# A merged stage of a graph layer: one more PSUM bank for the group's chain, paired product and rank tiles, a longer lead, and four-round turns without a barrier

## The chip, the cores and the metric

The kernel runs on one core of a Trainium2 chip. The metric is the device time of one execution in microseconds (us). The core has five engines that run their own instruction streams: PE (matrix multiply), DVE (vector), ACT (scalar and activation), POOL (GpSimd, which here issues indirect DMAs) and SP (which issues plain DMAs). They meet through semaphores alone. PE writes its results into PSUM, eight banks of 2 KB in each of 128 partitions; DVE and ACT read them from there.

## The reference

Two layers of a graph network over 32768 nodes with 256 features, and 524288 edges sorted by target:

```
# layer 0: attention inside blocks of 128 nodes (8 heads of 32), with residual
h  = relu(layernorm(x))
Q, K, V = (h @ W + b for W, b in ((Wq, bq), (Wk, bk), (Wv, bv)))
x  = x + softmax(Q @ K.T / sqrt(32) + edge_bias) @ V @ Wo + bo     # edge_bias lies in block 0 alone
# layer 1: one step of a gated graph layer, with residual
h  = relu(layernorm(x));  h = batchnorm(h)
a_in  = segment_sum((h @ W_in  + b_in )[src] * edge_weight[:, None],    dst)
a_out = segment_sum((h @ W_out + b_out)[dst] * edge_weight_n2[:, None], src)
xi, hh = concat(a_in, a_out) @ W_x2i + b_x2i,  h @ W_h2h
gate, new = sigmoid(xi[:, :256] + hh[:, :256]), tanh(xi[:, 256:] + hh[:, 256:])
x  = x + new + gate * (h - new)
```

The sums over edges are taken of the rows of h1 = relu(layernorm(x)) before the weights, which are applied afterwards.

## The kernel before

A first part of the program counts edges by block and builds tables of "items": an item is a window of 128 edges that have one target block of 128 nodes. Then comes the **merged stage**, which the change is about; after it, a stage that sums messages and rows by source and by target (`add_up`), and a last stage that computes the gates.

The merged stage does two things at once. One is layer 0: `project(g)` and `attend(g)` work on a group of four blocks (512 nodes). The other is to write, for every edge, the row of its target, scaled by the edge's weight, to the place that the edge has when sorted by source (`spread`, in three phases of edges, `PH`). Items are taken in rounds of 64 (`CI`). While a round runs, one group is attended and the next one projected; there are 64 groups, of which the first is done ahead.

For each item the steps are these (their lags in the table `steps`, line 1130, count items): `fetch` loads the target block's 128 rows `hb` from DRAM (SP). `spread_lanes` and `select` build a one-hot matrix `selT` from the edges' targets (PE, then DVE; once for four items), and `oh`, the one-hot of each edge's source block among 256 (DVE, one instruction for an item). `rank` (lines 1094 and 1096 to 1102) adds three bf16 products to a running count R in PSUM: `ones_b` with the oh of the item before, `triu` with that of two before, `tri` with its own. There are two tiles, R0 and R1, and items take them in turn. `place` (line 1114) is one DVE instruction that picks each edge's count out of R. `product` (line 1090) multiplies selT with hb into a tile `mp`, of which there are two. `scale` (line 1106, ACT) takes mp to SBUF with the edge's weight. `scatter` (line 1123, POOL) writes the 128 rows of 257 numbers and more to their places with an indirect DMA.

The **order** on PE, DVE, ACT and SP is that in which the Python loop over t emits instructions (`manual_schedule`, line 1139); POOL's is decided by the scheduler. At each t the loop emits the steps that are due by their lag and then what `project` and `attend` have registered for that t with the decorator `at(t)`. So their numbers are places in a common order: `at(B + 3)` stands behind the items' steps of t = B + 3. A wait is placed wherever an instruction needs a tile that another engine wrote, or writes a tile (or a PSUM bank) that another engine still reads.

PSUM is full: the group's chain has three tiles of one bank each, `sc`, `pt` and `mm`, which every part of project and attend shares; `bc` has one; mp two; R0 and R1 one each.

A **turn** is one passage of the hardware loop (`turns`, line 1135). Most turns hold four rounds (UG = 4), the rest of a phase takes turns of one round. At the end of a turn all engines meet at a barrier and their semaphores are reset. The loop of `add_up` does not do that: it is given `iteration_sync="staggered"`, its body is cut into four stages (`quarter`), and an engine may enter a stage when all have finished the stage before the last.

In the first phase there are five turns of four rounds, then turns of one round; in the second five; in the third four. Seven turns of one round have a group, and the last five have none.

Of the kernel before, what the change touches and what calls it, by code (L numbers as in the profile page):

```python
# [19 lines left out]
P = 128  # L20
# [479 lines left out]
def gnn_kernel(ctx, tc, x, src, dst, edge_attr, edge_type, w_in_e, w_out_e,  # L500
# [186 lines left out]
    with ExitStack() as c1:  # L687
# [56 lines left out]
        def project(g, qT, kbd):  # L744
# [7 lines left out]
            for b in range(GB):  # L752
# [7 lines left out]
                @at(17 + 2 * b)  # L760
                def _(b=b, row=row):
                    xn = row["xn"] = ab.tile([P, D], F32, name="xn")
                    nc.vector.tensor_scalar(xn, xg[:, b], mv[0][:, b, 0:1], rstd[0][:, b:b + 1],
                                            op0=ALU.subtract, op1=ALU.mult)

                @at(18 + 2 * b)
                def _(row=row):
                    row["tp"] = transposed("mm", row["xn"])

                @at(19 + 2 * b)  # L770
# [11 lines left out]
            for m in range(KC):  # L782
                ps = {}
                mc = slice(m * P, (m + 1) * P)
                bank = ("pt", "mm")[m]
                for k in range(KC):
                    @at(26 + 7 * m + k)
                    def _(m=m, k=k, ps=ps, mc=mc, bank=bank):
                        if k == 0:
                            ps["q"] = a_ps.tile([P, GN], F32, name=bank)  # L790
                        nc.tensor.matmul(ps["q"], wq[:, k, mc], hT[:, k], start=(k == 0), stop=(k == KC - 1))

                    @at(29 + 7 * m + k)
                    def _(m=m, k=k, ps=ps, mc=mc, bank=bank):
                        if k == 0:
                            ps["k"] = a_ps.tile([P, GN], F32, name=bank)
                        nc.tensor.matmul(ps["k"], wk[:, k, mc], hT[:, k], start=(k == 0), stop=(k == KC - 1))

                @at(28 + 7 * m)
# [3 lines left out]
                for j in range(HC):  # L803
                    @at(31 + 7 * m + j // 2)
# [10 lines left out]
            for b, t, bank in ((0, 41, "pt"), (2, 59, "sc")):  # L815
                ps = {}
                for i in range(2):
                    @at(t + i)
                    def _(b=b, i=i, ps=ps, bank=bank):
                        if i == 0:  # L820
                            ps["v"] = a_ps.tile([P, 2, D], F32, name=bank)
# [8 lines left out]
            @at(63)  # L830
# [5 lines left out]
        def attend(g, qT, kbd, bias=None):  # L836

            todo, at = steps_of()
            for b in range(GB):
# [3 lines left out]
                for m in range(KC):  # L843
                    hs = slice(m * HC, (m + 1) * HC)

                    @at(B + 4 * m)
# [7 lines left out]
                    @at(B + 1 + 4 * m)  # L854
# [5 lines left out]
                    for j in range(HC):  # L860
                        @at(B + (2, 6)[m] + j // 2)
# [3 lines left out]
                        @at(B + (3, 7)[m] + j // 2)  # L865
# [5 lines left out]
                    @at(B + (6, 9)[m])  # L871
# [7 lines left out]
                    @at(B + 10 + m)  # L879
# [7 lines left out]
                @at(B + 12)  # L887
# [6 lines left out]
                @at(B + 13)  # L894
# [3 lines left out]
                @at(B + 14)  # L898
# [4 lines left out]
                @at(B + 15)  # L903
# [5 lines left out]
                @at(B + 16)  # L909
# [9 lines left out]
                @at(B + 17)  # L919
# [3 lines left out]
                @at(B + 18)  # L923
# [5 lines left out]
                for n, u in enumerate(range(bs.start, bs.stop)):  # L929
                    h = {}  # L930

                    @at(B + 18 + 2 * n)
# [3 lines left out]
                    @at(B + 19 + 2 * n)  # L936
                    def _(u=u, h=h):
                        h["tp"] = transposed("mm", h1g[:, u])

                    @at(B + 20 + 2 * n)  # L940
# [3 lines left out]
            @at(B + 17)  # L944
# [3 lines left out]
            @at(B + 19)  # L948
# [3 lines left out]
            @at(B + 21)  # L952
# [26 lines left out]
        NM = 8  # L979
        fp = c1.enter_context(tc.tile_pool(name="p_f", bufs=1))  # L980
        wp = c1.enter_context(tc.tile_pool(name="p_w", bufs=2))
        sp = c1.enter_context(tc.tile_pool(name="p_s", bufs=2))
        op = c1.enter_context(tc.tile_pool(name="p_o", bufs=8))
        ip = c1.enter_context(tc.tile_pool(name="p_i", bufs=NM))
        hp = c1.enter_context(tc.tile_pool(name="p_h", bufs=10))
# [3 lines left out]
        zm = fp.tile([P, T3 // P, MW], F32, name="zmsg")  # L989
        nc.vector.memset(zm, 0.0)  # L990
        nc.vector.memset(zm[:, :, FW:FW + 1], -1.0e6)
        eno = fp.tile([CI, T1], F32, name="eno")
        nc.gpsimd.iota(eno, pattern=[[1, T1]], base=0, channel_multiplier=0, allow_small_or_imprecise_dtypes=True)
        R = [p1.tile([P, NB], F32, name=f"R{i}") for i in range(2)]
# [12 lines left out]
        def spread(k, lo, hi):  # L1007
# [8 lines left out]
            nc.scalar.dma_start(msg_d[k][hi - lo:hi - lo + T3].rearrange("(p e) w -> p e w", p=P), zm)  # L1016
            for r in R:
                nc.tensor.matmul(r, cn["row0"], soff[k], start=True, stop=False, skip_group_check=True)
# [69 lines left out]
            def product(i, q, c, turn):  # L1088
                mp = turn["mp", i] = pp.tile([P, D], F32, name="mp")
                nc.tensor.matmul(mp, turn["sel", i // 4][:, q % 4], turn.pop(("hb", i)), start=True, stop=True)  # L1090

            def add(what, of, to, turn):
                oh = turn["oh", of]
                nc.tensor.matmul(R[to % 2], cn[what], oh, start=False, stop=False, skip_group_check=True)  # L1094
# [15 lines left out]
            def place(i, q, c, turn):  # L1110
# [3 lines left out]
                nc.vector.scalar_tensor_tensor(jk, cn["iota1"], c["ed"][:, 0, q:q + 1], R[i % 2], op0=ALU.is_equal,  # L1114
# [331 lines left out]
```

## Time and profile before

| | us |
|---|---|
| median of 3 runs | 17105.49 (17104.96 to 17109.16) |
| profiled execution | 19598.35 |
| its span, first to last instruction | 19596.6 |
| first round of the merged stage begins | 1058.6 |
| last round with a group ends | 9421.7 |
| last scatter of the merged stage | 10044.9 |
| sums by source and target | 10064 to 17439 |
| gates, to the end | 17439 to 19597 |
| mean granted TensorE clock | 0.887 of full speed |

The profiled execution is one execution with the profiler on, and is longer than the timed ones. Times inside it are counted from its first instruction. In the page's part with the busy times, each engine has its busy time, its share of the span and its number of instructions; PEld is the loading of weights, which overlaps PE. The rows of digits cut the span in 40 slices, and PEclk is the clock that was granted, in tenths. A row of stretches gives, after the stretch and its length, the busy time and number of instructions of PE, PEld, DVE, ACT and POOL, then the granted clock, the share of the DMA engines and GB/s. A row of the waits names the waiting instruction and what released it, the total in us, how often, and the longest. A row in order of time gives start, duration, engine, line, operation, and in brackets the idle time before it with what ended that.

A round begins where the copies of line 1067 stand. Inside a turn of four rounds they are some 116, 122 and 129 us apart, and from the fourth round to the next turn's first some 152; turns of one round take 142 to 155 us with a group and 123 to 130 without.

### The profile page before, as it was taken

The numbers are of one execution on the slowest core, as the hardware profiler recorded it, in microseconds if no ns is written. First come the engines' busy times: TensorE is split into PE (matmuls) and PEld (weight loads), VectorE is DVE, ScalarE is ACT, GpSimd is POOL, SyncE is SP. The second block draws the span as 40 slices with busy tenths as digits, with TensorE's granted clock in tenths as the row PEclk, the third lists the DMA queues.
The fourth block names the chain that finished last, engine by engine and source line by source line (L and its number), as shares of the span: only waits on it lengthen the run. The fifth ranks groups of instructions, "written<-read, shape, count | busy, mean of one in ns | idle before, by whom it ended". The sixth has DMA issues, their size and how long they took to land. (4 is left out here: it accounts for less than half of the span.)

```text
span 19596.6 us, 292930 instructions
## 1 busy us (share of the span) xinstructions
PE 14917.0 (76%) x71786; PEld 10574.5 (54%) x71786; DVE 10035.6 (51%) x33823; ACT 6877.9 (35%) x17011; POOL 9326.3 (48%) x9309
## 2 busy tenths in 40 slices
PE   2078777777887777887668778777877777788889
PEld 2055555555555555555446666666666666653334
DVE  8656666566666656665444444444444444432222
ACT  0044444444444444444223333333333333320000
POOL 0045555445455445554555555555555555542222
PEclk6589989889888888988779999899999999999999
DMA  2044444444444434444446777677776777773332
GB/s 65 6 136 149 147 149 149 137 140 147 142 149 146 139 124 144 143 147 139 132 142 194 193 197 196 184 197 198 196 194 187 196 196 197 197 155 113 105 112 96
DMA packets 1829641, 2975.64 MB, mean 152 GB/s; under 512 B 299498, under 2 KB 1288135, under 8 KB 1827670
## 3 DMA queue, kind: packets, MB, share of 16 engines
q1 hardware_dynamic: 1203190, 1584.46, 27.5%
q0 software_dynamic: 430768, 1160.40, 20.5%
q10 hardware_dynamic: 194096, 212.95, 3.5%
q8 instruction: 590, 9.67, 0.2%
q14 instruction: 997, 8.17, 0.1%
HBM read 2124.16 MB, written 1248.64 MB: 172 GB/s over the span
## 5 line engine op out<-in xcount | busy, mean ns | idle before, releaser
L1123 POOL DMA_INDIRECT msg_d<-msg,pi x4352 | 4308.2, 990 | 3816.3 <-ACT msg L1106 1527.1
L1252 POOL DMA_INDIRECT rows<-h_d,ixc x3584 | 3407.5, 951 | 2331.8 <-issue 743.4
L1114 DVE SCALAR_TENSOR_TENSOR jk<-iota,edc,R 128x256 f32<-128x256 bf16 x4352 | 2072.8, 476 | 3059.3 <-remote 928.6
L1287 ACT ACTIVATE selo<-lane_row,sl 128x128 f32<-128x128 f32 x5040 | 1661.6, 391 | 4691.3 <-DVE sl L1284 1574.9
L1294 PE MATMUL ps_o<-m,selo 128*128 128x257 f32 x10080 | 2757.9, 413 | 645.7 <-ACT selo L1288 293.7
L1106 ACT ACTIVATE msg<-mp,edc 128x256 f32<-128x256 f32 x4352 | 2048.1, 477 | 3415.4 <-PE mp L1090 1522.5
L1266 PE MATMUL ps_i<-rows,sel 128*128 128x257 f32 x8960 | 2617.6, 412 | 761.6 <-DVE acc L1270 381.2
L1090 PE MATMUL mp<-hb,selT 128*128 128x256 f32 x8704 | 2926.6, 421 | 342.1 <-ACT msg L1106 145.7
L1294 PEld LDWEIGHTS ps_o<-m,selo 128*128 128x128 f32 x10080 | 1969.6, 205 | 1050.9 <-issue 312.5
L1266 PEld LDWEIGHTS ps_i<-rows,sel 128*128 128x128 f32 x8960 | 1627.5, 205 | 1054.7 <-DVE acc L1270 429.3
L1259 DVE TENSOR_SCALAR sel<-lane_row,ed 128x128 f32<-128x128 f32 x4480 | 1395.9, 360 | 973.2 <-PE idle L1267 374.7
L1090 PEld LDWEIGHTS mp<-hb,selT 128*128 128x128 f32 x8704 | 1460.2, 210 | 570.5 <-ACT msg L1106 230.9
L1094 PE MATMUL R<-oh,ones_b 128*128 128x256 bf16 x4352 | 1275.4, 293 | 635.6 <-issue 318.5
L1298 DVE SCALAR_TENSOR_TENSOR acc<-acc,blk,ps_o 128x257 f32<-128x257 f32 x1680 | 805.5, 479 | 1412.9 <-PE ps_o L1294 571.2
L1086 DVE TENSOR_SCALAR oh<-iota,edc 128x256 bf16<-128x256 bf16 x4352 | 1360.0, 313 | 2.0
L1094 PE MATMUL R<-oh,triu 128*128 128x256 bf16 x4352 | 1273.4, 293 | 10.5 <-DVE jk L1114 10.5
L1094 PE MATMUL R<-oh,tri 128*128 128x256 bf16 x4352 | 1272.2, 292 | 0.0
L1270 DVE SCALAR_TENSOR_TENSOR acc<-acc,blk,ps_i 128x257 f32<-128x257 f32 x2240 | 1070.0, 478 | 300.3 <-DMA sin_d<-acc 76.8
L1252 POOL DMA_INDIRECT rows<-h_d,ixh x896 | 852.2, 951 | 635.7 <-issue 247.2
L1284 DVE TENSOR_SCALAR sl<-m,blk 128x3 f32<-128x3 f32 x1680 | 416.6, 248 | 1372.4 <-DMA m<-msg_d 1139.5
L1094 PEld LDWEIGHTS <-triu 128*128 128x128 bf16 x4352 | 447.7, 103 | 1163.8 <-issue 1017.5
L1288 ACT ACTIVATE selo<-selo,one 128x384 f32<-128x384 f32 x1680 | 1031.1, 614 | 52.2
(372 smaller groups left out, 21051.9 us busy)
## 6 DMA issues: line engine op xcount, KB each, us to landing
m<-msg_d SPq DMA_DIRECT2D x1680, 396.0 KB
hb<-h_d SPq DMA_DIRECT2D x4352, 128.0 KB
sin_d<-acc SPq DMA_DIRECT2D x2240, 128.5 KB
sout_d<-acc SPq DMA_DIRECT2D x1680, 128.5 KB
msg_d<-msg,pi POOLq DMA_INDIRECT x4352
more<-sout_d ACTq DMA_DIRECT2D x128, 514.0 KB
rows<-h_d,ixc POOLq DMA_INDIRECT x3584
xg<-in_x SPq DMA_DIRECT2D x65, 512.0 KB
```

What stands on the lines that cost most here:

```text
L1086: nc.vector.tensor_scalar(oh, cn["iota1"], c["ed"][:, 0, q:q + 1], None, op0=ALU.is_equal)
L1090: nc.tensor.matmul(mp, turn["sel", i // 4][:, q % 4], turn.pop(("hb", i)), start=True, stop=True)
L1094: nc.tensor.matmul(R[to % 2], cn[what], oh, start=False, stop=False, skip_group_check=True)
L1106: nc.scalar.activation(msg[:, q % 4, 0:D], turn.pop(("mp", i)), AF.Copy, scale=c["ed"][:, 1, q:q + 1])
L1114: nc.vector.scalar_tensor_tensor(jk, cn["iota1"], c["ed"][:, 0, q:q + 1], R[i % 2], op0=ALU.is_equal, op1=ALU.mult, accum_out=c["pf"][:, q ...
L1123: s = nc.gpsimd.indirect_dma_start(out=msg_d[k][:], out_offset=bass.IndirectOffsetOnAxis(ap=c["pi"][:, j:j + 1], axis=0), in_=msgs[i // 4 ...
L1252: nc.gpsimd.indirect_dma_start(out=rows[(2 * i + r) % NR][:, 0:D], out_offset=None, in_=h1_d[:], in_offset=bass.IndirectOffsetOnAxis(ap=(i ...
L1259: nc.vector.tensor_scalar(sel[:, r], cn["lane_row"], c["ed"][:, 0, r, i:i + 1], c["ed"][:, 1, r, i:i + 1], op0=ALU.is_equal, op1=ALU.mult)
L1266: nc.tensor.matmul(ps, sel[:, r], rows[(2 * i + r) % NR], start=(r == 0), stop=(r == 1))
L1270: nc.vector.scalar_tensor_tensor(acc[0][i % NA], acc[0][(i - 1) % NA], c["blk"][:, 0, i:i + 1], c.pop(("t_ps", i)), op0=ALU.mult, op1=ALU.add)
L1287: nc.scalar.activation(sel[:, r], cn["lane_row"], AF.Abs, bias=sl[:, r:r + 1])
L1294: nc.tensor.matmul(ps, sel[:, r], m[:, r, 0:FW], start=(r == 0), stop=(r == T3 // P - 1))
```

## The change

It has five parts, all in the merged stage.

1. The group's chain gets a fourth PSUM tile, `mx`. The transposes of xn and h1g, and q, k and v of `project` use it; sc, pt and mm stay with attend. The numbers in `at()` are spread: between an instruction and the one on another engine that needs it there are now two steps where there was mostly one: sc at B + 5m (was 4m), av at B + 12 + m (was 10), o at B + 14 (was 12), its transposes at B + 16 (was 13), wo at B + 19 (was 15), x1g at B + 20 (was 16), std at B + 21, h1g at B + 23 + 3n (was 18 + 2n), its transposes at B + 25 + 3n, and k of project at 31 + 10m (was 29 + 7m).
2. mp becomes a tile for two items with two buffers (four items in two banks), and R0 and R1 become the halves of one tile in one bank. That is where the bank for mx comes from.
3. Items lead by 12 steps rather than 8: `LEAD`. There are 14 buffers for hb, not 10, and 7 for oh, not 8.
4. Turns of four rounds use the staggered form, with stage boundaries at each round's fourth step and without the hint for the branch. Turns of one round keep the barrier and the hint.
5. The row of zeros behind each phase's messages is kept once and broadcast by its DMA (three in all), and R is started by one matmul of 512 columns, not two of 256.

```diff
-                @at(17 + 2 * b)
+                @at(13 + 3 * b)
                 def _(b=b, row=row):
                     xn = row["xn"] = ab.tile([P, D], F32, name="xn")
...
-                @at(18 + 2 * b)
+                @at(15 + 3 * b)
                 def _(row=row):
-                    row["tp"] = transposed("mm", row["xn"])
+                    row["tp"] = transposed("mx", row["xn"])
...
-                    @at(26 + 7 * m + k)
-                    def _(m=m, k=k, ps=ps, mc=mc, bank=bank):
+                    @at(27 + 10 * m + k)
+                    def _(m=m, k=k, ps=ps, mc=mc):
                         if k == 0:
-                            ps["q"] = a_ps.tile([P, GN], F32, name=bank)
+                            ps["q"] = a_ps.tile([P, GN], F32, name="mx")
...
-            for b, t, bank in ((0, 41, "pt"), (2, 59, "sc")):
+            for b, t in ((0, 47), (2, 67)):
...
-            @at(63)
+            @at(67)
             def _():
                 nc.gpsimd.tensor_add(xb, xg, bo_b[:, None, :].to_broadcast([P, GB, D]))
...
-                        @at(B + (3, 7)[m] + j // 2)
+                        @at(B + 4 + 5 * m + j // 2)
                         def _(m=m, j=j, s=s):
                             if j == 0:
                                 s["pt", m] = a_ps.tile([P, HC, P], F32, name="pt")
...
-                @at(B + 16)
+                @at(B + 20)
                 def _(b=b, s=s):
                     nc.vector.tensor_add(x1g[:, b], s["y"], xb[:, b])
...
-                        h["tp"] = transposed("mm", h1g[:, u])
+                        h["tp"] = transposed("mx", h1g[:, u])
...
+        LEAD = 12
-        op = c1.enter_context(tc.tile_pool(name="p_o", bufs=8))
+        op = c1.enter_context(tc.tile_pool(name="p_o", bufs=7))
-        hp = c1.enter_context(tc.tile_pool(name="p_h", bufs=10))
+        hp = c1.enter_context(tc.tile_pool(name="p_h", bufs=14))
...
-        R = [p1.tile([P, NB], F32, name=f"R{i}") for i in range(2)]
+        R = p1.tile([P, 2, NB], F32, name="R")
...
             def product(i, q, c, turn):
-                mp = turn["mp", i] = pp.tile([P, D], F32, name="mp")
+                if i % 2 == 0:
+                    turn["mp"] = pp.tile([P, 2, D], F32, name="mp")
+                mp = turn["mp", i] = turn["mp"][:, i % 2]
...
-                nc.tensor.matmul(R[to % 2], cn[what], oh, start=False, stop=False, skip_group_check=True)
+                nc.tensor.matmul(R[:, to % 2], cn[what], oh, start=False, stop=False, skip_group_check=True)
...
-            steps = ((0, fetch), (4, spread_lanes), (6, select), (8, rank), (8, product), (8, place), (9, scale), (9, scatter))
+            steps = ((0, fetch), (LEAD - 4, spread_lanes), (LEAD - 2, select), (LEAD, rank), (LEAD, product), (LEAD, place),
+                     (LEAD + 1, scale), (LEAD + 1, scatter))
...
-                with tc.For_i(begin_at, end, nr, hint_engines=ENGINES) as it:
+                several = nr > 1
+                with tc.For_i(begin_at, end, nr, **({"iteration_sync": "staggered"} if several else {"hint_engines": ENGINES})) as it:
...
+                            if several:
+                                quarter(t, [0] + [i * CI + 3 for i in range(1, nr)], last + 1)
```

## The prediction

> **What bounds the kernel now.** I read the granted clock first (0.887), then the page's slices, the stretches, the chain, PE's waits, and last the order of time inside one round. The merged stage lies from 1058 us (its first round's copies) to 10045 us (its last scatter). Two lines of the page and one stretch, two steady rounds inside a turn, give its balance:
>
> ```profile
> PE 14917.0 (76%) x71786; PEld 10574.5 (54%) x71786; DVE 10035.6 (51%) x33823; ACT 6877.9 (35%) x17011; POOL 9326.3 (48%) x9309
> PEclk6589989889888888988779999899999999999999
> 1200.00:1460.00 260.00, 210.06 (x1156) 141.81 (x1155) 165.76 (x612) 122.76 (x307) 133.85 (x133) 0.91 0.48 152
> ```
>
> PE is busy 81% of the 260 us, DVE 64%, ACT 47%, POOL 51%: PE bounds the stage, with holes, and no second engine is near its limit. POOL sends scatters 1.29 us apart (0.99 busy, 0.30 issue) where an item takes about 2 us. The chain that ended last shows only the final stage (1% in all), so it says nothing here; the holes must be read from PE's waits over the 63 rounds with groups:
>
> ```profile
> PE R L1094 <- DVE jk L1114: 280.4, 201, 7.1
> PE R L1094 <- issue: 219.6, 116, 5.2
> PE sc L849 <- PEq L1135: 191.2, 15, 17.1
> PE pt L869 <- issue: 154.9, 90, 3.2
> PE mp L1090 <- ACT msg L1106: 136.4, 161, 2.3
> PE mm L741 <- DVE xn L763: 127.7, 39, 5.8
> PE mp L1090 <- issue: 93.5, 132, 2.4
> ...
> PE mp L1090 <- ACT kbd L810: 61.8, 56, 1.8
> ```
>
> ("issue" is a wait whose release the trace did not keep; an instruction's "issue" rows are counted with its named ones.) Three families: the rank waiting for the place (280.4 + 219.6 = 500 us), the barrier (191), and the links of the group's chain and of the product (L741 311 us with its smaller rows, L869 272, L1090 292: 875 us). Inside a round, at full clock:
>
> ```profile
> 1612.07 0.27 PE L1094 MATMUL R<-oh,ones_b 128*128 128x256 bf16 x1
> ...
> 1612.29 0.27 PE L1094 MATMUL R<-oh,tri 128*128 128x256 bf16 x1
> ...
> 1612.39 0.60 PE L1090 MATMUL mp<-hb,selT 128*128 128x256 f32 x2
> ...
> 1612.60 0.48 DVE L1114 SCALAR_TENSOR_TENSOR jk<-iota,edc,R 128x256 f32<-128x256 bf16 x1 [1.31 <-PE R L1094]
> ...
> 1612.83 0.27 PE L1094 MATMUL R<-oh,ones_b 128*128 128x256 bf16 x1
> ...
> 1613.00 0.08 DVE L1114 DVE_READ_ACCUMULATOR jk<-iota,edc,R 128x1 f32 x1
> ```
>
> An item costs PE 0.76 us (12.07 to 12.83). DVE's place starts 0.04 us after the rank's last matmul and is done at 13.08, 1.01 us after the rank began. Here the next rank began 0.25 us before that: it writes the other R tile.
>
> **Pages against the trace.** "PSUM — Partial Sum Buffer", section "PSUM bank collisions raise a hardware error", says that two engines on one bank and the same partitions at once are an error, whatever columns they touch, so that such instructions are ordered. In the rows above PE writes one R tile while DVE reads the other, which is allowed as they lie in different banks. The changed kernel puts both halves in one bank, and its built program does what the page says: a rank's first matmul waits for the place of the item just before, where it now waits for the one two back. The forecast goes by the page. The second is "TensorE: Matmul & The Clock Gate", Part 1: PE falls to half clock after an idle window of about 3.4 us. The trace agrees: after the 10.84 us hole at a turn's end the first R matmul (at 1588.00) takes 0.40 us, and one at 1589.61 takes 0.27. I take no gain from it in the sum.
>
> **The change part by part** (profiled execution, 19598.35 us, span 19596.6).
>
> 1. *Longer links in project and attend, and the bank mx.* xn to its transposes was one step and is two; exp to transposes likewise; h1g, o and wo likewise; xn, q, k, v and h1 get a bank that attend's mm, pt and sc do not share. The work itself is the same. The product's two buffers become two pairs: by the built program the even product waits for the scale three items back, the odd one for no scale. These are the 875 us. With the lock of part 2 DVE is at most one step behind PE, so a DVE link two steps long is met without a wait. ACT may be three behind and keeps its 1.28 us table loads and its waits for DVE's kbd (430.7 us on ACT), and the first steps of a turn have no items to cover a link. I keep a third: -583 us. From both sides: -780 (only a tenth stays) and -437 (half stays).
>
> 2. *R in one bank.* Lower side of the cost: a rank can follow the one before by 1.09 us at the soonest (1.01 and 0.04 to each side) instead of 0.76. In the turns' 4011 neighbours 955 are closer than 1.1 us, by 260 us together. Upper side: item by item the larger of PE's work, DVE's work and 1.1 us, which sums to 120.5 us a round, against PE's own 102.9 (both from the trace's durations between ranks and between places): 17.6 us a round. In between stands what each place really allows, as DVE may begin its step while PE is still in the step before: the sum of 1.09 plus DVE's work less PE's work of two steps, where positive. It is 11.7 us a round; with three steps, today's case, 0.6. With the changed order of steps (work lists of both programs, 13.1 against 14.3) it becomes 10.7. Today's waits are 500/63 = 7.9, so 7.3 a round come from lateness that such sums miss (DVE held by its own links); half of it goes with part 1. After: 10.7 + 3.7 = 14.4 a round, 907 us over 63 rounds: +407 us.
>
> 3. *No barrier between turns of four rounds.* 14 such turns in three runs of 5, 5 and 4, so 11 edges. Today an edge leaves PE idle for 10.84 us:
>
> ```profile
> 1570.12 0.37 PE L1094 MATMUL R<-oh,triu 128*128 128x256 bf16 x1 [0.21 <-DVE jk L1114]
> 1581.32 2.07 PE L849 MATMUL sc<-kbd,qT 128*128 128x512 f32 x2 [10.84 <-PEq L1135]
> ```
>
> The next stage's loop already passes its edge by stages, and there PE has a hole of 5.11 us:
>
> ```profile
> 10621.30 0.39 PE L1267 MATMUL idle<-lane_row,sel 128*128 128x128 f32 x2
> 10626.80 2.94 PE L1294 MATMUL ps_o<-m,selo 128*128 128x257 f32 x6 [5.11 <-ACT selo L1288]
> ```
>
> So 11 x 5.7 = -63 us. The hint for the branch goes with the barrier; its price is inside that 5.11. The stage waits stand 14 steps behind each boundary, when the awaited work is long done: nothing. They are also in POOL's and SP's queues. POOL may lag 32 items by its eight message buffers, less than the 50 steps allowed.
>
> 4. *Lead of 12, seven oh, 14 hb.* SP issues the same DMAs (hb 128 KB each), four steps earlier against the product; 14 buffers against 12 leave SP two steps ahead, as 10 against 8 did. SP's xg load now stands behind POOL's xb, one step after the last x1g: 0.42 + 2.35 + about 4.5 us to landing (issued at 2225.2, first bn_stats on it at 2229.7) is under 4 steps, and seven are there; if that cover goes, DVE stalls at bn_stats, and R with it. A scatter now waits for the one five back, not eight: 5 x 1.29 = 6.45 us, and at the edge everything landed within 6.4 us. A loop of one round keeps its barrier and has four more steps in which only the group works: about 1 us each (at 1581 to 1588 eight such steps take 6.7 us), 12 turns: +48 us, with 0 and +100 as ends.
>
> 5. *The zero row by broadcast, R's start in one matmul:* three DMAs and three matmuls: nothing.
>
> Sum: -583 + 407 - 63 + 48 = -191 us, 19407 us. The median of the runs is 17105.49, 0.873 of the profiled execution; I scale: 17105.49 x (1 - 191/19598) = 16940 us. What is late next is the place: rank, place, rank in turn.
>
> **Rivals.**
>
> A. *The lock becomes the bound: slower.* The upper side of part 2, 17.6 + 7.3 = 24.9 us a round, 1569 in all: +1069. Half of part 1's waits only move to the rank: -437. With -63 and +48: +617 us, 17645 us. For it: DVE's place starts over 0.55 us late in half of the items, so it is often the later one. Against it: DVE is busy 64% only. It decides once R's waits grow by over 568 us, 9 us a round.
>
> B. *More gain.* Part 1 at -780, R at +200, edges and loops as above, and, with no hole over 3.4 us, fewer stretches at half clock (0.92 over a turn; all of it would be some 32 us in 500, I take 200 us in all): -795 us, 16410 us. Against it: R's 955 close pairs.
>
> C. *No change.* The waits change their names and the stage still takes 126 us a round: PE's holes are what DVE and ACT need. Within 34 us of 17105.
>
> **How the numbers follow.** A run of this kernel repeats within some 0.03%, and 0.2% (34 us) is about what can be told from nothing. My forecast has 0.42, its own range 16700 to 17090 us; A 0.34, B 0.14, C 0.10. Faster: 0.42 x 0.95 + 0.14 = 0.54; same 0.10 + 0.01; slower 0.35. The range takes in most of A and of B: 16450 to 17520 us.
>
> **What would show it.** Right: L741, L869 and L1090 waits of PE fall from 875 to some 300 us; R's rise from 500 to some 900; neighbouring ranks are never under 1.05 us apart; PE's hole between turns is near 5 us; single-round loops grow by a few us. Wrong: R's waits over 1100 us (A) or under 600 (B); new waits at bn_stats for xg, or of PE for hb; POOL's rows with waits over its 0.30.

## The result, and the profile after

The changed kernel takes 17181.65 us (17138.02 to 17198.54, 8 runs) against 17101.49 us before: a ratio of 1.0044 [1.0033, 1.0055]. It is slower by some 75 us (80 between the medians), where 165 us less was forecast. The measured time lies inside the range, on the side of rival A.

The kernel before took 17100 us on one chip, 17290 on others and 19400 to 19570 on two more, with the profiler or without it. So it was not the profiler that made the execution longer from which the prediction was read: that profile has the 19.5 ms level, while the verdict and the changed kernel's profile have the 17.1 ms level. A profile of the kernel before near the verdict's level came later (run before_b below, 17295 us). Its waits of PE over the merged stage (1060 to 9300 us; waiting row, what released it, us in total, times, longest):

```profile
PE sc L849 <- PEq L1135: 218.6, 15, 19.8
PE pt L869 <- ACT pr L863: 170.9, 220, 1.9
PE mp L1090 <- ACT msg L1106: 167.4, 144, 1.8
...
PE R L1094 <- DVE jk L1114: 118.7, 112, 2.3
PE mm L741 <- DVE xn L763: 114.2, 117, 1.4
PE mm L741 <- ACT h1g L934: 82.0, 62, 3.2
```

The same view of the changed kernel:

```profile
PE R L1097 <- DVE jk L1117: 672.3, 899, 2.5
...
PE bc L1080 <- DVE selT L1085: 62.6, 26, 5.1
PE sc L848 <- PEq L1140: 51.3, 5, 14.6
PE pt L868 <- ACT pr L862: 35.4, 38, 1.9
```

Call PE's waits inside the group's chain and at the product the links (mm at 741, pt at 869, mp at 1090). With their smaller rows they come to 600 us before and to 50 after; the rank's wait for the place goes from 119 to 672 us. The links' waits are gone, and the rank waits for as long in their stead. In order of time, one item of the changed kernel (start, duration, engine):

```profile
2604.77 0.27 PE L1097 MATMUL R<-oh,ones_b 128*128 128x256 bf16 x1
...
2604.99 0.27 PE L1097 MATMUL R<-oh,tri 128*128 128x256 bf16 x1
...
2605.30 0.48 DVE L1117 SCALAR_TENSOR_TENSOR jk<-iota,edc,R 128x256 f32<-128x256 bf16 x1 [0.43 <-PE R L1097]
2605.70 0.08 DVE L1117 DVE_READ_ACCUMULATOR jk<-iota,edc,R 128x1 f32 x1
2605.84 0.27 PE L1097 MATMUL R<-oh,ones_b 128*128 128x256 bf16 x1
```

Rank, place, next rank stand strictly in turn, 1.07 us apart. Of all 4351 neighbours none is under 1.05 us; before, 1329 were, down to 0.76. The page of the kernel before at this level and of the changed one, with the busy times and the clock:

```profile
PE 14054.8 (81%) x71786; PEld 10157.9 (59%) x71786; DVE 10092.8 (58%) x33823; ACT 6860.6 (40%) x17011; POOL 9321.6 (54%) x9309
...
PEclk6589999999999999999889999999999999999999
```

```profile
PE 14133.3 (82%) x71780; PEld 10281.3 (60%) x71780; DVE 10222.2 (60%) x33823; ACT 6748.4 (39%) x17011; POOL 9315.0 (54%) x9309
...
PEclk6579999989999989999889999999999999999999
```

The clock hardly differs; PE is busy 79 us longer. A short stretch does not show the difference: 260 us inside a turn, 1200 to 1460 us, of the kernel before and of the changed one (stretch, length, then PE, PEld, DVE, ACT, POOL, clock, DMA, GB/s):

```profile
1200.00:1460.00 260.00, 230.81 (x1358) 158.53 (x1357) 191.70 (x703) 139.08 (x351) 152.79 (x153) 0.97 0.54 171
```

```profile
1200.00:1460.00 260.00, 229.77 (x1335) 163.96 (x1334) 191.23 (x694) 132.30 (x344) 153.49 (x153) 0.95 0.54 172
```

PE is busy 89% there (230.81 of 260), not 81% as in the profile of the prediction: the holes that the change could close are little more than half as wide.

The rows of waits do not hold the whole price. Here are all 63 rounds with a group, from the begin of the first to the begin of the next round after them, in before_b and in the changed kernel:

```profile
1057.47:8379.89 7322.42, 6177.79 (x36050) 4255.04 (x36050) 5180.38 (x18877) 3793.66 (x9525) 4200.78 (x4160) 0.94 0.51 164
```

```profile
1073.57:8417.78 7344.21, 6272.30 (x36048) 4424.94 (x36049) 5288.01 (x18876) 3698.55 (x9524) 4193.19 (x4160) 0.94 0.51 163
```

PE is idle for 73 us less (1145 and 1072 us), and busy for 94 us more. Yet its matmuls' own durations sum to much the same (11727 and 11742 us): they overlap less. Added up from the trace, the part of the rank's first matmul (ones_b) that no earlier matmul covers grows by 255 us, while each still lasts 0.28 us: it now often starts on an empty PE, as it has waited for the place. And holes under 150 ns, which the rows of waits leave out, grow from 18 to 100 us.

### The profile page after: what moved, and what is told of

It reads as the page before. It is cut to its first block, busy times and chain, and to the rows that moved or that the text cites. A ratio compares the mean times of both kernels' runs of the same rounds, so it can differ in the third digit from the quotient of the medians.

```text
span 17162.3 us, 294157 instructions
## 1 busy us (share of the span) xinstructions
PE 14133.3 (82%) x71780; PEld 10281.3 (60%) x71780; DVE 10222.2 (60%) x33823; ACT 6748.4 (39%) x17011; POOL 9315.0 (54%) x9309
## 5 line engine op out<-in xcount | busy, mean ns | idle before, releaser
L1109 ACT ACTIVATE msg<-mp,edc 128x256 f32<-128x256 f32 x4352 | 2005.2, 476 | 3497.6 <-PE mp L1093 3181.6
L1273 PE MATMUL ps_i<-rows,sel 128*128 128x257 f32 x8960 | 2502.0, 398 | 334.8 <-DVE acc L1277 244.3
L1301 PE MATMUL ps_o<-m,selo 128*128 128x257 f32 x10080 | 2566.0, 392 | 203.4 <-ACT selo L1295 201.0
L1093 PE MATMUL mp<-hb,selT 128*128 128x256 f32 x8704 | 2716.4, 395 | 3.5 <-DMA hb<-h_d 3.5
L1301 PEld LDWEIGHTS ps_o<-m,selo 128*128 128x128 f32 x10080 | 1866.7, 194 | 513.5 <-ACT selo L1295 179.2
L1273 PEld LDWEIGHTS ps_i<-rows,sel 128*128 128x128 f32 x8960 | 1562.9, 198 | 587.3 <-DVE acc L1277 364.3
L1097 PE MATMUL R<-oh,ones_b 128*128 128x256 bf16 x4352 | 1217.1, 280 | 796.4 <-DVE jk L1117 672.3
L1093 PEld LDWEIGHTS mp<-hb,selT 128*128 128x128 f32 x8704 | 1371.6, 199 | 69.9 <-DMA hb<-h_d 5.7
L1097 PE MATMUL R<-oh,tri 128*128 128x256 bf16 x4352 | 1219.3, 280 | 0.0
L1097 PE MATMUL R<-oh,triu 128*128 128x256 bf16 x4352 | 1206.5, 278 | 0.0
```

Source lines behind the costliest of these rows:

```text
L1097: nc.tensor.matmul(R[:, to % 2], cn[what], oh, start=False, stop=False, skip_group_check=True)
L1109: nc.scalar.activation(msg[:, q % 4, 0:D], turn.pop(("mp", i)), AF.Copy, scale=c["ed"][:, 1, q:q + 1])
L1273: nc.tensor.matmul(ps, sel[:, r], rows[(2 * i + r) % NR], start=(r == 0), stop=(r == 1))
L1301: nc.tensor.matmul(ps, sel[:, r], m[:, r, 0:FW], start=(r == 0), stop=(r == T3 // P - 1))
```

## The experiments

The theory that came out of the traces (L): the lock of R's two halves in one bank takes what the longer links give. Rivals: the edges by stages or the longer lead cost what is lost (E); waits at the links and at the rank are one and the same lost time, so that each only moves into the other (M).

Each kernel was timed beside the kernel before on the same chip. Ratios are to it, with the 95% interval; the level is the median of the kernel before there. PE's waits are sums over 1060 to 9300 us, "links" those at the rows of lines 741, 869 and 1090 or what stands for them. Durations of turns are counted from the begins of rounds: 14 turns of four, 7 of one round with a group.

| run | level | ratio | rank's wait | links | turn of four | its last round | turn of one |
|---|---|---|---|---|---|---|---|
| kernel before (before_b) | 17289 | 1 | 119 | 600 | 456.9 | 132.6 | 132.3 |
| changed (after_again) | 17120 | 1.0040 [1.0025, 1.0056] | 672 | 50 | 457.8 | 131.8 | 135.6 |
| changed, barrier back (barrier) | 17120 | 1.0078 [1.0064, 1.0092] | 668 | 43 | 466.0 | 141.4 | 136.9 |
| changed, lead 8 (lead8) | 17289 | 1.0038 [1.0024, 1.0052] | 736 | 21 | 459.4 | 132.0 | 130.4 |
| changed, no lock, no mx (two_R_b) | 17289 | 0.9841 [0.9827, 0.9854] | 312 | 189 | 436.0 | 123.8 | 131.2 |
| the same, lead 8 (two_R8) | 17108 | 0.9846 [0.9833, 0.9860] | 299 | 284 | 439.8 | 123.0 | 125.7 |
| the same, lead 8, barrier (links8) | 17108 | 0.9841 [0.9827, 0.9854] | 281 | 272 | 442.3 | 133.2 | 127.7 |
| the same, no pairs either (spread8_b) | 17286 | 0.9856 [0.9839, 0.9872] | 255 | 258 | 440.6 | 132.6 | 128.4 |
| before + one bank (one_bank_b) | 17289 | 1.0160 [1.0146, 1.0173] | 686 | 163 | 474.3 | 137.1 | 139.0 |
| before + lead 12 (lead) | 17120 | 1.0092 [1.0077, 1.0108] | 136 | 594 | 465.7 | 138.4 | 138.5 |
| before + pairs (pairs) | 17108 | 1.0060 [1.0046, 1.0074] | 104 | 648 | 463.6 | 133.6 | 134.5 |
| before + edges by stages (edges_b) | 17108 | 0.9986 [0.9979, 0.9993] | 37 | 723 | 453.8 | 123.0 | 131.3 |

The stage itself, round to last scatter, can be set beside each other across the two levels: what differs between 17100 and 17290 is the unchanged stage of sums (from its first to its last gather 6056 to 6095 us against 6249 to 6270).

### At 19570 us: the kernel before, and three edits

> The unchanged kernel once more, for a profile that isn't longer than the timed runs. Both theories: span near 17100 us. If the profiled execution that the prediction was read from was longer by a factor everywhere, PE's link waits (lines 741, 869, 1090: 875 us there) come out at 0.87 of that, some 760, and R's (500) at some 440. If it was longer by what only it had (semaphores seen late), both come out far smaller: links under 600 us and R under 350, with rounds inside a turn at some 105 to 115 us instead of 116 to 129, and the stage of sums at 6064 us as in the changed kernel.

19546.99 us, rounds inside a turn at 115 to 130 us, links 871 us, rank 517: the prediction's profile over again, and not the 17100 us that both theories expected. That profile was not an outlier.

> The kernel before with one edit: R0 and R1 as halves of one bank (and R started by one matmul). Theory L (the lock takes what the links give): PE's waits for the place at the rank rise by 300 to 500 us and the time by 200 to 500 us, 17300 to 17600. Theory E (the lock is small, and the loss lies at the edges and in the loops of one round): within 80 us of before.

```diff
-        R = [p1.tile([P, NB], F32, name=f"R{i}") for i in range(2)]
+        R2 = p1.tile([P, 2, NB], F32, name="R")
+        R = [R2[:, i] for i in range(2)]
```

1.0022 [1.0016, 1.0029], some 43 us, on theory E's side: the rank's wait rose from 517 to 1120 us, the links' fell from 871 to 156.

> The kernel before with one edit: turns of four rounds pass into each other by stages, no barrier. Theory L: faster by 30 to 90 us (11 edges of some 5.7 us). Theory E: slower by 50 to 150 us, since the stage waits and the missing branch hint cost more than the barrier did.

```diff
-                with tc.For_i(begin_at, end, nr, hint_engines=ENGINES) as it:
+                several = nr > 1
+                with tc.For_i(begin_at, end, nr, **({"iteration_sync": "staggered"} if several else {"hint_engines": ENGINES})) as it:
...
+                            if several:
+                                quarter(t, [0] + [i * CI + 3 for i in range(1, nr)], last + 1)
```

1.0071 [1.0059, 1.0084], 139 us more: theory E's side again.

> The changed kernel with R0 and R1 in two banks again and without the bank mx: the spread steps, the pairs, the lead of 12 and the edges by stages stay, and what used mx goes to pt, mm and sc where these are free (xn's transposes to pt and mm, q and k to sc, pt, mm, sc, v to pt, h1's transposes to sc and mm). Theory L: PE's waits at the rank fall from 796 us to under 350, and the time falls under both kernels, to 16650 to 16950 us. Theory E: it stays within 80 us of the changed kernel, 17100 to 17260.

```diff
-        R = p1.tile([P, 2, NB], F32, name="R")
+        R = [p1.tile([P, NB], F32, name=f"R{i}") for i in range(2)]
...
-                    row["tp"] = transposed("mx", row["xn"])
+                    row["tp"] = transposed("pt" if b < 2 else "mm", row["xn"])
...
-                            ps["q"] = a_ps.tile([P, GN], F32, name="mx")
+                            ps["q"] = a_ps.tile([P, GN], F32, name=("sc", "mm")[m])
-                            ps["k"] = a_ps.tile([P, GN], F32, name="mx")
+                            ps["k"] = a_ps.tile([P, GN], F32, name=("pt", "sc")[m])
-            for b, t in ((0, 47), (2, 67)):
+            for b, t in ((0, 47), (2, 62)):
-                            ps["v"] = a_ps.tile([P, 2, D], F32, name="mx")
+                            ps["v"] = a_ps.tile([P, 2, D], F32, name="pt")
...
-                        h["tp"] = transposed("mx", h1g[:, u])
+                        h["tp"] = transposed("sc" if u < GB - 1 else "mm", h1g[:, u])
```

1.0069 [1.0056, 1.0082], with 1083 us of waits at the rank although the lock is gone. Taken alone, these three would have buried theory L. But this level has another bound. DVE's waits for the place, over the same stretch, at 19545 us:

```profile
DVE jk L1114 <- PE R L1094: 848.6, 723, 3.4
DVE jk L1114 <- remote: 713.9, 169, 7.8
DVE jk L1114 <- PE mp L1090: 563.8, 303, 4.4
```

and in before_b, at 17293 us:

```profile
DVE jk L1114 <- PE R L1094: 1585.3, 1497, 3.1
```

At the 17.3 ms level the waits of the place, all but 2 us, are ended by the rank that it needs. At the 19.5 ms level 1280 us end with something later than that rank: a product, which the place does not need, or a release that the trace doesn't hold ("remote"). Measured from the end of the rank's last matmul, 810 of the 1801 waits of the place at 19545 us end over 0.3 us late, and none of the 1500 in before_b. The place itself takes 477 ns in both; PE's product takes 420 ns on average against 393, and the granted clock over the rounds is 0.89 against 0.94. Why releases of PE come late on some chips, and whether the lower clock is a cause of it or comes of the longer holes, no run here shows. What follows is that the verdict's level must be the experiments' level.

### The changed kernel, its edges, and the lead alone (17120 us)

> The changed kernel beside the kernel before, on one chip. The four runs before this one took some 19570 us for the kernel before, not 17100, as the profile did that the prediction was read from. Theory S (the level of time hangs on the chip, and the change's ratio with it): where the kernel before takes 19570 us the changed one comes out at a ratio of 1.007 to 1.015, above the 1.0044 measured at 17100, since both the edges by stages (1.0071) and the form without the lock (1.0069) lost there; where it takes 17100 us the ratio is 1.0044 again. Theory N (the level changes nothing of the ratio): 1.0033 to 1.0055 at either.

1.0040 [1.0025, 1.0056]: the verdict again, which both theories give for this level. The changed kernel was not run at 19.5 ms, so S and N are not told apart for it.

> The changed kernel with the barrier and the hint back in turns of four rounds; all else as changed. Theory E (the edges by stages cost more than the barrier): faster than the changed kernel by 60 us or more, and no slower than the kernel before, ratio 0.995 to 1.001. Theory L (the edges gain 63 us as forecast, the lock loses): slower than the changed kernel by 40 to 90 us, ratio to the kernel before 1.007 to 1.010.

17254.14 us, 70 us above the changed kernel beside it: theory L's side, and E's is excluded. All of PE's waits at the turns' first row (sc) are 239 us here and 82 us beside it, so less than half of that wait was lost time. PE's hole at a turn's end, in order of time, in before_b and in the changed kernel:

```profile
1513.12 1.22 PE L849 MATMUL sc<-kbd,qT 128*128 128x512 f32 x1 [13.23 <-PEq L1135]
```

```profile
1533.21 2.05 PE L848 MATMUL sc<-kbd,qT 128*128 128x512 f32 x2 [3.90 <-issue]
```

> The kernel before with the lead alone: items lead by 12 steps, 14 buffers for hb and 7 for oh (and the zero row kept once, which makes the room). The forecast has +48 us for the four more steps of the twelve turns of one round, between 0 and +100, and the fourteen turns of four rounds have the same four steps, which it left out: if these cost as much a turn, +104 us (ratio 1.006); if the longer lead hides more at the turn's start, 0 (1.000).

```diff
-            steps = ((0, fetch), (4, spread_lanes), (6, select), (8, rank), (8, product), (8, place), (9, scale), (9, scatter))
+            steps = ((0, fetch), (8, spread_lanes), (10, select), (12, rank), (12, product), (12, place), (13, scale), (13, scatter))
...
-        op = c1.enter_context(tc.tile_pool(name="p_o", bufs=8))
+        op = c1.enter_context(tc.tile_pool(name="p_o", bufs=7))
-        hp = c1.enter_context(tc.tile_pool(name="p_h", bufs=10))
+        hp = c1.enter_context(tc.tile_pool(name="p_h", bufs=14))
```

1.0092 [1.0077, 1.0108], +156 us: more than the expectation's +104. In the table: turns of one round +6.2 us (7 of them, +44), turns of four +8.8 (14, +123). At this barrier four more steps stand in front of a turn's first items and cost the full 8.8 us.

### Lock and lead apart (17289 us)

> The unchanged kernel, looked at for a profile of the 17100 us level. From the profile of the longer lead alone at that level (PE's waits at the rank 136 us, at the links of lines 741, 869 and 1091 594 us): R near 140 and the links near 600 us here, rounds inside a turn some 102, 112 and 112 us apart and the edge some 10 us shorter than with the longer lead.

As expected: rank 119, links 600.

> R0 and R1 as halves of one bank, all else as before. Theory L (the lock adds its waits to those there are): PE's waits at the rank rise from some 140 to over 600 us and the time by 300 to 500 us, 17400 to 17600. Theory M (the rank's wait takes the place of the waits at the links, since both end when DVE and ACT have come round): R's waits rise as much, those at lines 741, 869 and 1091 fall by nearly as much, and the time rises by 0 to 100 us, 17100 to 17200.

+277 us (0.0160 of 17289). PE's waits:

```profile
PE R L1095 <- DVE jk L1115: 686.3, 632, 4.1
PE sc L849 <- PEq L1136: 190.2, 15, 16.9
...
PE mm L741 <- DVE xn L763: 62.9, 63, 1.3
PE pt L869 <- ACT pr L863: 47.5, 98, 1.6
```

The rank's wait rises by 567 us, the links' fall by 437 (600 to 163), and the time rises by 277. Both theories have a part of it: nearly three quarters of the old waits at the links move behind the rank, as M has it, and the time is lost nevertheless, nearly as L has it. Over the 63 rounds, 290 us longer, PE is idle for 128 us more and busy for 162 us more, and as in the changed kernel it is the rank's first matmul that overlaps less (248 us). This edit is the lock alone, so the lock is shown to cost its time at this level.

> The changed kernel with R in two banks and without mx. Theory L: the lock's waits go, 400 us or more off the changed kernel: 16600 to 16780. Theory M: the steps of DVE and ACT bound the round as before, and other waits come in: 17000 to 17180, no more than 180 us under the changed kernel.

0.9841 [0.9827, 0.9854], 17014 us, faster than both kernels. PE's waits:

```profile
PE R L1097 <- DVE jk L1117: 312.1, 241, 3.0
PE bc L1080 <- DVE dlbc L1068: 148.7, 5, 35.7
PE pt L868 <- ACT kbd L809: 96.9, 63, 1.6
```

At a level of 17100 that would be 16830; against the changed kernel (1.0040 to 1.0044) it is 2.0% or some 345 us. Theory M allowed no more than 180; it falls. L asked for 400 and is a little too high.

> The changed kernel with the lead of 8 again (the group's steps stand one earlier and its last one two, so that they end inside the turn). The lead alone cost 156 us: 26 turns of four more steps at 1.5 us each. If that is a cost of its own, this one takes 156 us less than the changed kernel, 17028 us, ratio 0.994 to 0.998, and is faster than both. If the spread steps need the longer lead (a turn's first and last steps are filled by the group anyway), it stays within 40 us of the changed kernel.

```diff
-            @at(B + 28)
+            @at(B + 27)
...
-        LEAD = 12
+        LEAD = 8
...
-                                                todo.setdefault(t + u, []).extend(fs)
+                                                todo.setdefault(t + u - 1, []).extend(fs)
```

1.0038 [1.0024, 1.0052]: no different from the changed kernel. So the 156 us of the lead alone are not in the changed kernel. The stages in place of the barrier may be why a turn of four does not pay them, or the spread steps, which give its first steps other work: no run has lead 12 with the barrier and without the lock.

### Links, pairs, edges and lead without the lock (17108 us)

> The changed kernel with R in two banks, without mx, and with the lead of 8 (the two edits of two_R_b and lead8 together). two_R_b took 0.9841 of the kernel before. If a longer lead costs its steps whenever the lock doesn't hide them: 26 turns of four steps at 1.5 us, -156 us more, ratio 0.974 to 0.978. If the edges by stages hide them (as lead8 at 1.0038 beside 1.0044 hints): 0.981 to 0.984.

0.9846 [0.9833, 0.9860] at lead 8 beside 0.9841 [0.9827, 0.9854] at lead 12. Turns of one round get 5.5 us shorter (38 us in all), turns of four 3.8 us longer (53 us): the two nearly cancel.

> The same with the barrier back in turns of four rounds: the spread steps and the pairs alone. If the links are worth what PE waited for them (lines 741, 869, 1090: 600 us at this level): ratio 0.965 to 0.975. If half of it only moves to the rank or to other waits: 0.98 to 0.99. If the gain of two_R_b came from the edges: 0.995 to 1.0.

0.9841 [0.9827, 0.9854], 16834.96 us: the spread steps and the pairs alone are worth 272 us, near half of the links' 600, and the edges by stages add nothing here that can be measured. (The buffers for hb and oh and the kept row of zeros are those of the changed kernel too; PE's waits for hb were 0.9 us before and 0.6 here.) The profiled execution was this kernel's longest, 16888 us. Its PE's waits:

```profile
PE R L1097 <- DVE jk L1117: 277.9, 327, 2.7
PE sc L848 <- PEq L1140: 223.3, 15, 19.6
...
PE bc L1080 <- DVE selT L1085: 115.2, 172, 1.5
PE pt L868 <- ACT hT L772: 88.9, 63, 1.4
```

The links fall from 600 to 272 us, the rank's wait rises from 119 to 281, that for bc behind selT (both lines of bc) from 105 to 143. The pt row behind hT comes of giving up mx: transposes of xn lie in a bank that attend wants one step later. Over the 63 rounds, 236 us shorter, PE is idle for 144 us less and busy for 92 us less.

> The kernel before with one edit: mp as pairs. PE's waits for the scale (168 us at line 1090) go. If they were lost time: ratio 0.990 to 0.993. If another link ends them: 0.997 to 1.0, with more at lines 741 and 869 or at the rank.

```diff
-                mp = turn["mp", i] = pp.tile([P, D], F32, name="mp")
+                if i % 2 == 0:
+                    turn["mp"] = pp.tile([P, 2, D], F32, name="mp")
+                mp = turn["mp", i] = turn["mp"][:, i % 2]
```

1.0060 [1.0046, 1.0074]: neither of the two. The product's waits go from 168 to 1 us, those at pt and mm rise from 432 to 647 (and mm at 885 from next to nothing to 57), and 105 us are lost.

```profile
PE pt L869 <- ACT pr L863: 327.1, 254, 2.3
...
PE mm L741 <- ACT h1g L934: 126.3, 126, 3.7
```

A wait taken from the middle of a chain of links comes back at its next link, here with more. Why it comes back with more was not tried.

> The kernel before with one edit: turns of four rounds pass into each other by stages. From the changed kernel with and without the barrier (1.0040 and 1.0078 in one call): -65 us, ratio 0.995 to 0.998. If the stage waits hold engines back when the steps are short, as at the longer times of the first runs (1.0071): 1.002 to 1.008.

0.9986 [0.9979, 0.9993], -24 us: faster, by a little less than the first theory's range. The last round of a turn gets 9.6 us shorter, the three others 2.2 us longer each. At 19.5 ms the same edit cost 139 us.

> As links8 (lead of 8, barrier, R in two banks, no mx), but without the pairs: mp in two buffers for one item each, as before. So it is the kernel before with the spread steps and the banks that go with them. Pairs alone took 1.006, spread steps and pairs together 0.9841. If the two gain together only (with the spread steps in place the product's wait for the scale is what is left): 0.990 to 0.997, with 100 us or more at the product's line. If the spread steps are all of the gain: 0.978 to 0.985.

```diff
-                if i % 2 == 0:
-                    turn["mp"] = pp.tile([P, 2, D], F32, name="mp")
-                mp = turn["mp", i] = turn["mp"][:, i % 2]
+                mp = turn["mp", i] = pp.tile([P, D], F32, name="mp")
```

0.9920 [0.9907, 0.9934], which is the first theory's number, but at 19406 us, so it can't be set beside links8. At this level too the spread steps gain.

> The changed kernel with the bank taken from mp, not from R: R0 and R1 in two banks, mx kept, mp one pair in one bank. So the item's lock stands between the product (PE) and the scale (ACT) and no longer between the rank and the place (DVE). If it is the place of the lock that costs (the rank stands first in the item, right behind the place of the item before): PE's waits at the product stay under 300 us and the time is near that of the form without a lock, ratio 0.984 to 0.992. If any two items in one bank cost alike: 1.000 to 1.010, with 600 us or more of waits at the product.

```diff
-        pp = c1.enter_context(tc.tile_pool(name="p_ps", bufs=2, space=PSUM))
+        pp = c1.enter_context(tc.tile_pool(name="p_ps", bufs=1, space=PSUM))
...
-        R = p1.tile([P, 2, NB], F32, name="R")
+        R = [p1.tile([P, NB], F32, name=f"R{i}") for i in range(2)]
...
```

This is the changed kernel with R in two banks as in two_R, but with mx kept. 1.0372 [1.0358, 1.0387], also at 19406 us, slower than both of its theories, with this as PE's largest row:

```profile
PE mp L1093 <- ACT msg L1109: 1126.2, 673, 4.6
```

1673 us in all at the product. At that level a lock between product and scale is far dearer than R's was in one_bank (1.0022). At 17.1 ms it was not tried, so lock and mx stay together in the 345 us.

> The spread steps without the pairs once more: the run before it took 19400 us for the kernel before, where the ratio (0.992) can't be set beside those at 17100. At 17100: if the spread steps are all of the 1.6% of links8, ratio 0.981 to 0.987, PE's waits at the product below 100 us; if the pairs are needed for half of it, 0.989 to 0.995, with 150 us or more at the product.

0.9856 [0.9839, 0.9872] at 17286 us: the first theory. The intervals with pairs (0.9841) and without overlap; 230 us of waits at the product, over twice what that theory gave, cost nothing to speak of. The two runs show best that waits on one engine take each other's place: without the pairs PE waits for 230 us at the product and 13 at pt, with them for 1 and 232, and the time is the same.

## Why the prediction was wrong

The direction failed on one term. In us at the 17.1 ms level, with the forecast's terms times 0.873:

| step | forecast | measured |
|---|---|---|
| 1 longer links and pairs | -509 | -272 (links8) |
| 2 R in one bank (with mx) | +355 | +345 (after_again against two_R_b) |
| 3 no barrier | -55 | +9 without the lock, -24 alone, -70 in the changed kernel |
| 4 lead | +42 | -9 without the lock, 0 to +10 with it, +156 alone |
| 5 zero row, R's start | 0 | not seen |
| sum | -167 | -272 + 345 + 9 - 9 = +73; the kernel: +75 |

The measured sum is a walk from the kernel before by links8, two_R8 and two_R_b to the changed kernel, so it must come out at +75 within its noise: it places the loss, and is no test of it. The two 9s are within the noise. On the other walk, by one_bank_b and barrier, the lock comes first and costs 277 us, and behind it the longer links, mx, pairs and lead together give 140 (1.0160 to 1.0078), for -467 forecast: step 1 falls furthest short either way.

**Step 1, the failing one: the term of 875 us was mis-sized, and its "I keep a third" took PE's waits for lost time.** Two thirds of 875 us were to go, at no price elsewhere but in step 2. Of the 509 us that this makes at the verdict's level, 272 came. First, the 875 us belong to a chip on which PE's releases come late; near the level of the verdict (before_b) the same three families hold 600 us, and two thirds of that are 400. Scaling the sum by 0.873 (875 to 764) did not mend that: the links' waits shrank to 0.69, while the place kept its 477 ns and PE's product went to 0.93. Second, of the 328 us that left the links without the lock (links8), 162 appeared at the rank and 38 at bc. What was gained in time is in part no wait at all: over the rounds PE has 144 us less of idle time and 92 us less of busy time. The prediction let part 1 lower the rank's wait ("half of it goes with part 1"); links8 shows the rank's wait rising when the links are loosened, and pairs shows waits moving from one link to the next. In the changed kernel itself the links fell further than forecast, to 50 us against some 300. The rank, which stands first in each item, now holds PE longer, and a wait that vanishes behind a larger one is no gain.

**Step 2 was right in mechanism; in time its size came near, in waits it did not.** The minimum of 1.09 us between ranks is 1.07, and the order rank, place, rank is as read from the built program. The Trainium skill ("PSUM — Partial Sum Buffer", section "PSUM bank collisions raise a hardware error") says that two engines on one bank and the same partitions at once raise an error. Both programs keep clear of it: in the changed kernel none of the 4352 places overlaps a matmul on R, while in before_b, with two banks, 1962 do (on the other bank), and ranks follow at 0.76 us. (That the chip raises the error no run here shows.) The rank's wait was forecast to rise by 407 us, from 500 to 907; it rose by 553, from 119 to 672, and the overlap that its first matmul lost came on top. That the lock's time is near the forecast all the same (277 alone, 345 with mx, for 355) is partly luck: it is what is left after other waits went in behind the rank's. The alternative that was ruled out by "DVE is busy 64% only" is the one that holds the lesson: DVE is busy 74% here (191.70 of 260 us), and a lock asks whether each single place comes in time, not for the mean.

**Rival A** had the mechanism of the result, with its sum too high: 617 us for measured 75. Its turning point, 568 us more at the rank, was worked out against 583 us of links, with the signs of the edges and the loops turned round (583 + 63 - 48 is 598). Against the 272 that the links give, it lies far lower, and 553 was enough.

**Step 3** was right for the hole (5.1 us forecast, 3.90 in the row above; 13.23 before) and for the changed kernel (-70 side by side against -63). That the gain depends on what else bounds the turn's other rounds (nothing without the lock) it did not see.

**Step 4**: four more steps cost the turns of one round 5.5 to 6.2 us, 38 to 44 in all, against 48. The turns of four were left out; under the barrier, in the kernel before, they cost 123 us more; in the changed kernel they don't. bn_stats' wait for xg was no loss, as forecast: 68 us before, 49 after; PE's waits for hb are 3.5 us.

Beyond the steps: in the changed kernel the first round begins at 1073.7 us, 16 us later than in before_b (1057.6); forms without mx begin between 1050 and 1060, and swap_bank, with mx and without the lock on R, at 1076, so the delay goes with mx. With one bank for all of project there is less room where the group done ahead runs without items. That this is the cause was only argued. From the first round to the last scatter the changed kernel takes 7830 us against 7801. These two make 45 of the 75 us; the other 30 are not placed, as there is no profile of the kernel before at 17100 us.

## What to carry to other kernels

Before a sum is made of waits, make sure that the profile is of the level at which the time is measured: if the profiled execution is 15% above the timed runs, waits and work do not shrink by one factor. Waits of different rows on one engine are not additive: loosening one link gives back only what no other link, and no lock further up the item, was about to take. Nor are the waits the whole price of a lock: a matmul that has waited starts on an empty PE, and the overlap that it loses (some 250 us here) is booked as busy time, so compare busy and idle over the same work. And don't pay for slack with a bank that carries a two-engine handover per item: here the spread steps with the pairs were worth 272 us with the banks that there were, 16835 us against 17108, and the bank taken from R cost as much or more (277 us alone, 345 with mx).

## What was not expected of the hardware

The time of one program differs by 14% between chips (17100, 17290 and 19400 to 19570 us). As far as the chip is recorded, all but one were used a single time, so a state of the chip at that hour is not told apart from the chip itself. DVE's place takes 477 ns at each, PE's product 393 to 421 ns; on the longest, waits for PE are ended late or by an event that the trace doesn't name (714 us "remote" on DVE's place alone, none at 17.3 ms). An edit's sign can hang on it: the form without the lock is 1.6% faster at 17.3 ms and 0.7% slower at 19.6; the edges by stages -0.14% and +0.71%.
